# Group ends, norms and V's scaling on VectorE behind an attention's last unit, and two blocks of the next projection at a time

## The chip, the cores and the metric

The kernel runs on one core of one Trainium2 chip. The metric is the device time of one execution in microseconds (us), taken as the median of several runs.

## The reference

A network of four graph layers on one graph of 3327 nodes with 512 features. `adj` is sparse, with more neighbours for the nodes of low numbers. Every layer adds to x what it makes of the normed x:

```
h = max(layernorm(x), 0);  x = x + layer_l(h, adj)        # l = 0, 1, 2, 3
layers 0, 2, 3, attention with 8 heads of 64:
  Wh = h @ W;  e[i,j] = leaky_relu(s_dst[i] + s_src[j], 0.2) where adj[i,j] > 0
  out[i] = sum_j softmax_j(e[i,j]) * Wh[j]
  layer 0: out normed over the nodes, column by column, then relu;  layers 2, 3: elu(out)
layer 1, SAGE:
  agg = mean of h over the neighbours;  relu(([h W_self, agg W_nb] + b) @ W_comb + b_comb)
```

s_src and s_dst are products of Wh with two vectors for each head.

## The kernel before

The nodes are padded to 3328, which is 26 blocks of 128. A block has two groups of 64 destination rows, so there are 52 groups. For each group a list of neighbours is made once; a gather is an indirect DMA of 128 listed rows, issued by GpSimd.

**The attention** (`attend`, called for layers 0, 2 and 3) takes the groups in units of up to three gathers from the layer's `table`. A row of the table holds, for each head, V (64 numbers, already scaled with the exponential of the source's score) and that exponential itself, and the exponential for the other branch of the leaky relu. For a unit VectorE takes a maximum into PSUM (`mx`, L1266; three banks) and multiplies with the mask (`wgt`, L1273); TensorE then sums the weighted rows and their weights into `facc` (L1287). The first operand of the maximum, `r_bc` (L1198), comes from `r_dram` over `r_two` (L1190). The order of TensorE, VectorE and ScalarE within `attend` is by hand: instructions run in the order in which the program makes them. After each unit `later()` advances every open `ending` by one step, and calls `tick`.

An **ending** of a group copies its sums out of PSUM on ScalarE (`sums`, L1215), takes the reciprocal of the weights' sums on VectorE (`rd`, L1219), and multiplies on ScalarE, one head at a time (L1225), into `fhp`, or in layer 0 into `bn_y`. After a block's second group, `finish` follows: in layers 2 and 3 the elu and the sum with x (`fin_e` L1314, `fin_x` L1316 on ScalarE, L1318 and L1319 on VectorE, stored at L1320), then `proj.begin` for the next layer's projection. In layer 0, sums over the nodes follow (`bmean_ps` L1374, `bn_mean` L1376, `bn_d` L1401).

**SAGE** (layer 1) gathers rows of h (`z_rows`, issued at L1165), sums them with the mask on TensorE (`sage_acc`, L1522), and goes on with each block: scaled by the degree (`s_ag`, L1461), transposed (`a_ps` L1465, `aT` L1467), multiplied (`n_ps` L1471), `s_o` on VectorE (L1476, L1477), `proj.begin`. Here a scheduler orders the engines, after costs of its own.

**The next layer's projection** (`Following`) runs beside the layer before. `begin` opens a block's norm (`early`): sums and squares on ScalarE (`ln_j`, L782 and L784), the reciprocal root in short steps of both engines (L708 to L719), and `ln_h` on ScalarE (L792, L793). The other steps (`ready`) are `rest_by_rows` beside SAGE, and `rest` beside layer 2's attention. `rest`: four transposes (`p_ps` L845), `hT` with column sums on ScalarE (L848), the scores (`p_sd` L853; read at L857, L858, L860), `p_wh` (L866), V's scaling on ScalarE, one head at a time (L870), the store of the table's rows (L871), the transpose `p_tr` of the scores' exponentials (L874; halves at L730 to L734), and the store of `r_dram` (`r_row` L877, L879). `rest_by_rows` takes the scores from the products of `p_wh` (L808) with two vectors on VectorE (`sd_pr` L811, `sd_col` L813), scales V on VectorE (L824), and has `p_tr` at L831. `tick` advances the first open block by up to two steps; `drain` ticks until nothing is open. The PSUM tiles of `rest` share one bank (`pb=1`), those of `rest_by_rows` two. Layer 3's table is complete when `proj.drain()` ends behind `attend(2, ...)`, and layer 3's gathers come after it.

Of the kernel before, what the change touches and what calls it, by code (L numbers as in the profile page):

```python
# [23 lines left out]
F32 = mybir.dt.float32  # L24
# [8 lines left out]
ALU = mybir.AluOpType  # L33
# [5 lines left out]
P = 128  # L39
H = 8  # L40
F = 64
D = H * F
KC = D // P
BANK = 512
# [6 lines left out]
GB = 64  # L51
# [6 lines left out]
UNIT = 3  # L58
# [643 lines left out]
def rsqrt(nc, pool, cs, v, scale=1.0, bufs=3):  # L702


    n = v.shape[1]
    y = pool.tile([P, n], F32, name="rs_y", tag=f"rs_y{n}", bufs=bufs)
    g = pool.tile([P, n], F32, name="rs_g", tag=f"rs_g{n}", bufs=bufs)
    nc.scalar.activation(g, v, AF.Ln, scale=scale, bias=cs["eps"])  # L708
    nc.scalar.activation(y, g, AF.Exp, scale=-0.5)

    def step():
        h = pool.tile([P, n], F32, name="rs_h", tag=f"rs_h{n}", bufs=bufs)
        nc.vector.tensor_scalar(h, v, -0.5 * scale, -0.5 * EPS, ALU.mult, ALU.add)
        if n == 1:
            nc.vector.tensor_scalar(g, y, y, h, ALU.mult, ALU.mult)
        else:
            nc.vector.tensor_tensor(g, y, y, ALU.mult)
            nc.vector.tensor_tensor(g, g, h, ALU.mult)
        nc.vector.scalar_tensor_tensor(y, g, 1.5, y, ALU.add, ALU.mult)  # L719
        return y  # L720

    return step
# [17 lines left out]
class Following:  # L740
# [3 lines left out]
    def __init__(self, tc, cs, N, wl, W, WA, table, r_dram, pool, psum, pb=1, ab=None):  # L744

        self.__dict__.update(locals())
        nc = tc.nc
        if ab is not None:
            self.ab = pool.tile([P, 2, D], F32, name=f"ab{wl}")
            for k, a in enumerate(ab):  # L750
                nc.sync.dma_start(self.ab[:, k, :], a.partition_broadcast(P))
        self.NB = table.shape[0] // P
        self.Wt = pool.tile([P, KC, D], F32, name=f"fWt{wl}")
        nc.sync.dma_start(self.Wt, W.rearrange("(kc p) o -> p kc o", p=P))
        self.hs = pool.tile([P, self.NB, KC], F32, name=f"hs{wl}")
        self.early, self.ready = [], []

    def begin(self, c, xt):
        self.early.append(self.norm(c, xt))

    def tick(self):
        for _ in range(min(2, len(self.ready))):
            while self.ready and next(self.ready[0]) is None:
                self.ready.pop(0)
        for g in list(self.early):
            hx = next(g)
            if hx is not None:
                self.early.remove(g)
                self.ready.append((self.rest if self.ab is None else self.rest_by_rows)(*hx))
# [3 lines left out]
            self.tick()  # L773

    mean = Projection.mean

    def norm(self, c, xt):
        nc, pp, cs = self.tc.nc, self.pool, self.cs
# [62 lines left out]
    def rest(self, c, hx):  # L841
        nc, pp, WA, wl = self.tc.nc, self.pool, self.WA, self.wl
        tp = self.psum.tile([P, KC, P], F32, name="p_ps", tag="p_ps", bufs=self.pb)
        for kc in range(KC):
            nc.tensor.transpose(tp[:, kc, :], hx[:, kc * P : (kc + 1) * P], self.cs["ident"])  # L845
        hT = pp.tile([P, KC, P], F32, name="hT", tag="hT", bufs=2)
        for kc in range(KC):
            nc.scalar.activation(hT[:, kc, :], tp[:, kc, :], AF.Relu, accum_out=self.hs[:, c, kc : kc + 1])  # L848
        yield True
        self.mean(c, hT)  # L850
        sd = self.psum.tile([P, BANK], F32, name="p_sd", tag="p_ps", bufs=self.pb)
        for kc in range(KC):
            nc.tensor.matmul(sd[:, : 2 * H], hT[:, kc, :], WA[wl][:, kc, :], start=(kc == 0), stop=(kc == KC - 1))  # L853
        row = pp.tile([P, ROW], F32, name="v_row", tag="v_row", bufs=2)
        V = row[:, : H * (F + 1)].rearrange("p (h f) -> p h f", f=F + 1)
        d = sd[:, H : 2 * H]
        nc.scalar.activation(V[:, :, F : F + 1], d.rearrange("p (h o) -> p h o", o=1), AF.Exp)  # L857
        nc.scalar.activation(row[:, H * (F + 1) :], d, AF.Exp, scale=-0.8, bias=self.cs["down"])  # L858
        sf = pp.tile([P, H], F32, name="s_col", tag="s_col", bufs=2)
        nc.scalar.copy(sf, sd[:, :H])  # L860
        yield True

        nc.vector.tensor_scalar(sf, sf, -SMALL, SMALL, ALU.max, ALU.min)
        wh = self.psum.tile([P, D], F32, name="p_wh", tag="p_ps", bufs=self.pb)
        for kc in range(KC):
            nc.tensor.matmul(wh, hT[:, kc, :], self.Wt[:, kc, :], start=(kc == 0), stop=(kc == KC - 1))  # L866
        yield True
        rs = halves(nc, pp, self.cs, sf)
        for h in range(H):
            nc.scalar.mul(V[:, h, 0:F], wh[:, h * F : (h + 1) * F], V[:, h, F : F + 1])  # L870
        nc.sync.dma_start(self.table[c * P : (c + 1) * P, :ROW], row.bitcast(I32))  # L871
        yield True
        tr = self.psum.tile([2 * H, P], F32, name="p_tr", tag="p_ps", bufs=self.pb)
        nc.tensor.transpose(tr, rs(), self.cs["ident"])  # L874
        yield True
        rr = pp.tile([2 * H, P], F32, name="r_row", tag="r_row", bufs=2)
        nc.scalar.copy(rr, tr)  # L877
        n = P // GB
        nc.sync.dma_start(  # L879
            self.r_dram[c * n : (c + 1) * n, :, :, :].rearrange("g t h i -> (t h) g i"),  # L880
            rr.rearrange("h (g i) -> h g i", i=GB),
        )
        yield None
# [253 lines left out]
def sparse(ctx: ExitStack, tc: tile.TileContext, t: dict, out: bass.AP, WA, ls, cs, idx, rdeg, first):  # L1137
# [29 lines left out]
        )  # L1167


    def attend(layer, table, r_dram, finish, tick=lambda: None, home=None):  # L1170

# [8 lines left out]
        with tc.tile_pool(name=f"fatt{layer}", bufs=2) as ap, tc.tile_pool(  # L1182
            name=f"facc_ps{layer}", bufs=2, space=PSUM
        ) as aps, tc.manual_schedule(engines={ET.PE, ET.DVE, ET.Activation}):
            rows, rrs, rbs, accs, ends = {}, {}, {}, {}, []

            def fetch(g):
                if g < ls.G:
# [12 lines left out]
            def ending(g, hps={}):  # L1201

                b, u = divmod(g, PG)
                if u == 0:
                    hps[b] = home[:, b, :] if home is not None else None
                    if home is None:
                        hp_ = ap.tile([P, D], F32, name="fhp", tag="hp", bufs=3)
                        hps[b] = hp_
                hp, o0 = hps[b], u * GB
                fin = finish(b, hp, ap)  # L1210
                if u == PG - 1:
                    next(fin)
                yield
                sm = ap.tile([P, sw], F32, name="sums", tag="sums", bufs=4)
                nc.scalar.copy(sm, accs.pop(g)[:, :sw])  # L1215
                sm = sm.rearrange("p (q x) -> p q x", x=F + 1)
                yield
                rd = ap.tile([P, hq, 1], F32, name="rd", tag="rd", bufs=4)
                nc.vector.reciprocal(rd, sm[:, :, F : F + 1])  # L1219
                yield  # L1220
                for v in range(PG):
                    mine = slice(v * GB, (v + 1) * GB)
                    for q in range(hq):
                        h = q * PG + v
                        nc.scalar.mul(hp[o0 : o0 + GB, h * F : (h + 1) * F], sm[mine, q, 0:F], rd[mine, q, :])  # L1225
                yield
                if u == PG - 1:
                    del hps[b]
                    yield from fin
# [31 lines left out]
            for i, (g, k0, n, begins, stops) in enumerate(units):  # L1261
# [31 lines left out]
                            )  # L1293
                if stops:
                    ends.append(ending(g))
            while ends:
                later()

    def following(lx, layer, wl, W, pb=1, ab=None):
# [7 lines left out]
    def elu_into(xin, dst, then=lambda c, xt: None):  # L1307
        def finish(c, hp, pool):
            k = used(c) if dst is out else P
            xr = pool.tile([P, D], F32, name="fin_x", tag="fin_x", bufs=4)  # L1310
            nc.sync.dma_start(xr, xin[c * P : (c + 1) * P, :])
            ex = pool.tile([P, D], F32, name="fin_e", tag="fin_e", bufs=2)
            yield
            nc.scalar.activation(ex, hp, AF.Exp)  # L1314

            nc.scalar.activation(xr, xr, AF.Identity, bias=cs["less"])  # L1316
            yield
            nc.vector.scalar_tensor_tensor(xr, hp, 0.0, xr, ALU.max, ALU.add)  # L1318
            nc.vector.scalar_tensor_tensor(xr, ex, 1.0, xr, ALU.min, ALU.add)  # L1319
            nc.sync.dma_start(dst[c * P : c * P + k, :], xr[:k, :])  # L1320
            then(c, xr)

        return finish
# [206 lines left out]
    with ExitStack() as l3:  # L1530
        at2 = proj
        proj = following(l3, 3, 2, t["L3_gnn_W"])
        attend(2, at2.table, at2.r_dram, elu_into(x2, x3, proj.begin), proj.tick)
        proj.drain()
    attend(3, proj.table, proj.r_dram, elu_into(x3, out))


# [85 lines left out]
```

## Time and profile before

| what | value |
|---|---|
| median of three runs | 2559.43 us (2559.01 to 2560.68) |
| the profiled execution | 2553.76 us, span 2551.8 us, mean granted TensorE clock 0.851 |
| busy in the span | TensorE 1825.0 us, VectorE 1852.3 us, ScalarE 1068.3 us, GpSimd 1387.4 us |
| layer 0's end: sums read on ScalarE to `bn_mean` | 803.47 to 808.1 us |
| SAGE with the projection beside it | some 937 to 1445 us |
| join of layers 2 and 3: last attention matmul to layer 3's first gather | 1998.3 to 2046.5 us |
| layer 3's end: sums read on ScalarE to the last output step | 2532.65 to 2538.1 us |

The page shows one execution. A time in a timeline is in microseconds from the start of its span. Groups of instructions are shown as the source line, engine, operation and tile, then busy time, mean nanoseconds of one, the idle time of the engine in front of them, and what ended that idle time. PE is TensorE, PEld its weight loads, DVE VectorE, ACT ScalarE, POOL GpSimd, SP the engine that issues most DMAs. Block numbers in brackets, as in `p_wh`(23), count from 0 to 25.

### The profile page before, as it was taken

How to read it: one execution, taken by the hardware profiler on the slowest of the kernel's cores; microseconds unless marked ns; L12 is line 12 of the kernel's file. 1: busy time of each engine (PE TensorE's matmuls, PEld its weight loads, DVE VectorE, ACT ScalarE, POOL GpSimd, SP SyncE). 2: the span in 40 equal slices, each digit the busy share in tenths (PEclk: the TensorE clock that was granted, in tenths of full speed). 3: DMA queues.
4: the chain of work that ended last, by engine and by line, in shares of the span. 5: the costliest groups of instructions: out<-in, count | busy, mean ns of one | idle time of the engine just before them, and what ended most of it. 6: DMA issues, size and time to landing. Idle time of an engine off the chain costs nothing.

```text
span 2551.8 us, 53690 instructions
## 1 busy us (share of the span) xinstructions
PE 1825.0 (72%) x21112; PEld 1161.8 (46%) x21112; DVE 1852.3 (73%) x2272; ACT 1068.3 (42%) x3810; POOL 1387.4 (54%) x1482
## 2 busy tenths in 40 slices
PE   3667756776677698889999657778878646566653
PEld 2444444454454342223333356656555435555543
DVE  7667579999997850222333499999877279999996
ACT  4553212333445332334455214667766601233444
POOL 1000176777772026777777277776554067777672
PEclk9767889988888899999999778897877787777787
DMA  8773198888783566788888478887665178888784
GB/s 326 288 263 123 43 296 276 280 281 260 241 253 95 191 217 198 234 247 260 254 267 255 125 223 242 235 240 232 199 200 177 39 215 232 236 238 243 232 238 123
DMA packets 189057, 562.57 MB, mean 220 GB/s; under 512 B 37764, under 2 KB 42304, under 8 KB 185470
## 3 DMA queue, kind: packets, MB, share of 16 engines
q0 software_dynamic: 115456, 404.86, 53.3%
q1 hardware_dynamic: 73342, 154.20, 17.0%
q8 instruction: 169, 2.77, 0.4%
q14 instruction: 90, 0.74, 0.1%
HBM read 499.26 MB, written 59.68 MB: 219 GB/s over the span
## 4 chain that ended last, share of the span: by engine, by line
PE 30%; DVE 24%; issue 13%; ACT 9%; DMA 8%; POOL 3%; DVEq 0%; SPq 0%; POOLq 0%; ACTq 0%
DVE mx L1266 12%; PE facc L1287 8%; DVE wgt L1273 8%; PE sage_acc L1522 4%; DMA z_rows<-h_dram,idx 4%; PE p_wh L866 4%; DMA rows<-table,idx 3%; PE n_ps L1471 3%; PE p_wh L808 3%; ACT fhp L1225 2%; POOL z_rows L1165 2%; PE s_ps L1445 2%; POOL rows L1165 1%; ACT bn_y L1225 1%; ACT v_row L870 1%
## 5 line engine op out<-in xcount | busy, mean ns | idle before, releaser
L1165 POOL DMA_INDIRECT rows<-table,idx x1077 | 1027.7, 954 | 580.0 <-issue 224.5
L1287 PE MATMUL facc<-rows,wgt 128*64 128x65 f32 x17232 | 722.5, 253 | 393.7 <-DVE wgt L1273 259.7
L1287 PEld LDWEIGHTS facc<-rows,wgt 128*64 128x64 f32 x17232 | 667.1, 165 | 518.2 <-DVE wgt L1273 310.5
L1266 DVE TENSOR_TENSOR mx<-r_bc,rows 128x1536 f32<-128x1536 f32 (+1 forms) x405 | 639.4, 1579 | 48.4 <-DMA fin_x<-fx 17.7
L1273 DVE TENSOR_TENSOR wgt<-mx,mask 128x1536 f32<-128x1536 f32 (+1 forms) x405 | 638.4, 1576 | 42.3 <-DVE mx L1266 1.0
L1165 POOL DMA_INDIRECT z_rows<-h_dram,idx x359 | 340.7, 949 | 273.7 <-ACT hT L1442 141.0
L1225 ACT ACTIVATE fhp<-sums,rd 64x64 f32<-64x64 f32 x832 | 219.9, 334 | 305.4 <-DVE rd L1219 302.0
L1522 PE MATMUL sage_acc<-z_rows,z_mask 128*64 128x512 f32 x718 | 209.8, 618 | 33.0 <-DMA z_rows<-h_dram,idx 32.6
L1258 ACT ACTIVATE mask<-on 128x192 uint8<-128x192 uint16 (+1 forms) x135 | 46.5, 345 | 325.3 <-DVE on L1252 321.8
L1086 POOL DMA_DIRECT2D list_b<-shift x12 | 6.0, 503 | 271.7 <-DVE shift L1040 271.5
L811 DVE TENSOR_TENSOR sd_pr<-p_wh,ab 128x1024 f32<-128x1024 f32 x26 | 31.8, 1225 | 141.4 <-PE p_wh L808 141.4
L1522 PEld LDWEIGHTS sage_acc<-z_rows,z_mask 128*64 128x64 f32 x718 | 52.2, 137 | 156.2 <-issue 77.6
L680 PE MATMUL wh_ps<-fWt,hT 128*128 128x512 f32 x208 | 123.3, 748 | 0.0
L866 PE MATMUL p_wh<-fWt,hT 128*128 128x512 f32 x208 | 117.2, 714 | 1.4 <-ACT s_col L860 1.4
L1225 ACT ACTIVATE bn_y<-sums,rd 64x64 f32<-64x64 f32 x416 | 109.5, 333 | 2.4 <-DVE rd L1219 0.5
L1503 ACT CAST z_mask<-mask 128x128 f32<-128x128 uint8 (+1 forms) x196 | 52.7, 284 | 118.7 <-PE sage_acc L1522 117.5
L1476 DVE TENSOR_TENSOR s_o<-n_ps,bn_y 128x512 f32<-128x512 f32 x26 | 17.9, 690 | 116.2 <-PE n_ps L1471 116.2
L1215 ACT COPY sums<-facc 128x260 f32<-128x260 f32 x156 | 56.6, 363 | 104.7 <-DMA rows<-table,idx 77.7
L1471 PE MATMUL n_ps<-fWx,aT 128*128 128x512 f32 x208 | 98.7, 608 | 0.0
L808 PE MATMUL p_wh<-fWt,hT 128*128 128x512 f32 x208 | 96.9, 610 | 2.0 <-DVE hT L699 1.9
L1445 PE MATMUL s_ps<-fWx,hT 128*128 128x512 f32 x208 | 93.5, 603 | 3.4 <-ACT hT L1442 3.4
L1198 PE MATMUL r_bc<-r_two,fones 2*128 2x512 f32 x156 | 89.1, 575 | 6.6 <-DMA r_two<-r_dram 3.6
(213 smaller groups left out, 2146.3 us busy)
## 6 DMA issues: line engine op xcount, KB each, us to landing
adj_i<-in_adj SPq DMA_DIRECT2D x26, 1664.0 KB
table<-v_row SPq DMA_DIRECT2D x78, 264.0 KB
rows<-table,idx POOLq DMA_INDIRECT x1077
fin_x<-fx SPq DMA_DIRECT2D x52, 256.0 KB
ln_x<-in_x SPq DMA_DIRECT2D x26, 256.0 KB
bn_x<-in_x SPq DMA_DIRECT2D x13, 512.0 KB
fx<-bn_x SPq DMA_DIRECT2D x13, 512.0 KB
fsage_x<-fx SPq DMA_DIRECT2D x26, 256.0 KB
```

Of the source, the lines that this page charges most:

```text
L680: nc.tensor.matmul(wh, hT[:, kc, :], self.Wt[:, kc, :], start=(kc == 0), stop=(kc == KC - 1))
L808: nc.tensor.matmul(wh, hT[:, kc, :], self.Wt[:, kc, :], start=(kc == 0), stop=(kc == KC - 1))
L866: nc.tensor.matmul(wh, hT[:, kc, :], self.Wt[:, kc, :], start=(kc == 0), stop=(kc == KC - 1))
L1165: nc.gpsimd.indirect_dma_start(out=dst, out_offset=None, in_=src[:, :], in_offset=bass.IndirectOffsetOnAxis(ap=idx[:, k : k + 1], axis=0))
L1198: nc.tensor.matmul(rb, ones[0:2, :].bitcast(F32R), rrs.pop(g).bitcast(F32R), start=True, stop=True)
L1225: nc.scalar.mul(hp[o0 : o0 + GB, h * F : (h + 1) * F], sm[mine, q, 0:F], rd[mine, q, :])
L1266: nc.vector.tensor_tensor(mx[:, :n], rbs[g].unsqueeze(1).to_broadcast(full), gt[:, :n, H * (F + 1) : ROW].unsqueeze(3).to_broadcast(full), ...
L1273: nc.vector.tensor_tensor(wt[:, :n], mx[:, :n], mk.unsqueeze(2).to_broadcast(full), ALU.mult)
L1287: nc.tensor.matmul(accs[g][v * GB : (v + 1) * GB, q * (F + 1) : (q + 1) * (F + 1)], wt[:, k, h, :], gt[:, k, h * (F + 1) : (h + 1) * (F + 1)],
L1445: nc.tensor.matmul(ps, hT[:, kc, :], Wx[:, 0, kc, :], start=(kc == 0), stop=(kc == KC - 1))
L1471: nc.tensor.matmul(ps, aT[:, kc, :], Wx[:, 1, kc, :], start=(kc == 0), stop=(kc == KC - 1))
L1522: nc.tensor.matmul(acc[u * GB : (u + 1) * GB, :], m, z, start=f, stop=l)
```

## The change

Behind the last unit of an attention, endings that have not yet read their sums do all of their work on VectorE: a reciprocal straight from PSUM and two products with a broadcast operand, one for each half of the partitions. `begin` takes a norm from VectorE's column statistics (`norm_by_columns`) where the projection has `ab`, which is the one beside SAGE, for all its blocks, or where the spare banks are open. In the attention of layer 2, which now gets the projection as `beside`, one more tile of the maxima's three banks is taken behind the last unit and given to the projection (`hurry`): `p_sd`, `p_wh` and `p_tr` then go to its banks 0, 1 and 2, `tick` advances each of up to two open blocks by one step, and V is scaled by one product on VectorE. The projection's remaining steps run in `attend`'s last loop, within its order by hand, in place of `proj.drain()`.

```diff
     def begin(self, c, xt):
-        self.early.append(self.norm(c, xt))
+        self.early.append((self.norm_by_columns if self.spare is not None or self.ab is not None else self.norm)(c, xt))
+    def busy(self):
+        return self.early or self.ready
+    def hurry(self, spare):
+        self.spare = spare
+    def bank(self, shape, name, k):
+        if self.spare is not None:
+            return self.spare[: shape[0], k, : shape[1]]
+        return self.psum.tile(shape, F32, name=name, tag="p_ps", bufs=self.pb)
     def tick(self):
+        if self.spare is not None:
+            for g in self.ready[:2]:
+                if next(g) is None:
+                    self.ready.remove(g)
+            self.step()
+            return
         for _ in range(min(2, len(self.ready))):
             while self.ready and next(self.ready[0]) is None:
                 self.ready.pop(0)
+        self.step()
...
+    def norm_by_columns(self, c, xt):
+        nc, pp, cs = self.tc.nc, self.pool, self.cs
+        st = pp.tile([P, nc.vector.BN_STATS_DIM], F32, name="ln_st", tag="ln_st", bufs=2)
+        nc.vector.bn_stats(st, xt)
+        mv = pp.tile([P, nc.vector.BN_AGGR_DIM], F32, name="ln_mv", tag="ln_mv", bufs=3)
+        nc.vector.bn_aggr(mv, st)
+        step = rsqrt(nc, pp, cs, mv[:, 1:2])
+        yield
+        y = step()
+        if c == self.NB - 1:
+            nc.vector.tensor_tensor(y, y, cs["real"], ALU.mult)
+        hx = pp.tile([P, D], F32, name="ln_h", tag="ln_h", bufs=3)
+        nc.vector.tensor_scalar(hx, xt, mv[:, 0:1], y, ALU.subtract, ALU.mult)
+        yield c, hx
...  rest():
-        sd = self.psum.tile([P, BANK], F32, name="p_sd", tag="p_ps", bufs=self.pb)
+        sd = self.bank([P, BANK], "p_sd", 0)
...
-        wh = self.psum.tile([P, D], F32, name="p_wh", tag="p_ps", bufs=self.pb)
+        wh = self.bank([P, D], "p_wh", 1)
...
-        for h in range(H):
-            nc.scalar.mul(V[:, h, 0:F], wh[:, h * F : (h + 1) * F], V[:, h, F : F + 1])
+        if self.spare is not None:
+            nc.vector.tensor_tensor(
+                V[:, :, 0:F], wh.rearrange("p (h f) -> p h f", f=F), V[:, :, F : F + 1].to_broadcast([P, H, F]), ALU.mult
+            )
+        else:
+            for h in range(H):
+                nc.scalar.mul(V[:, h, 0:F], wh[:, h * F : (h + 1) * F], V[:, h, F : F + 1])
...
-        tr = self.psum.tile([2 * H, P], F32, name="p_tr", tag="p_ps", bufs=self.pb)
+        tr = self.bank([2 * H, P], "p_tr", 2)
...  attend(..., beside=None), in ending():
+                if over:
+                    sm = accs.pop(g)[:, :sw].rearrange("p (q x) -> p q x", x=F + 1)
+                    rd = ap.tile([P, hq, 1], F32, name="rd", tag="rd", bufs=4)
+                    nc.vector.reciprocal(rd, sm[:, :, F : F + 1])
+                    for v in range(PG):
+                        mine = slice(v * GB, (v + 1) * GB)
+                        nc.vector.tensor_tensor(
+                            hp[o0 : o0 + GB, :].rearrange("p (q v f) -> p q v f", v=PG, f=F)[:, :, v, :],
+                            sm[mine, :, 0:F],
+                            rd[mine].to_broadcast([GB, hq, F]),
+                            ALU.mult,
+                        )
+                    if u == PG - 1:
+                        del hps[b]
+                        yield from fin
+                    return
...
-            while ends:
+            over.append(True)
+            if beside is not None:
+                mx = aps.tile([P, UNIT, H, GB], F32, name="mx", tag="mx", bufs=1)
+                beside.hurry(mx.rearrange("p k h i -> p k (h i)"))
+            while ends or (beside is not None and beside.busy()):
                 later()
...
-        attend(2, at2.table, at2.r_dram, elu_into(x2, x3, proj.begin), proj.tick)
-        proj.drain()
+        attend(2, at2.table, at2.r_dram, elu_into(x2, x3, proj.begin), proj.tick, beside=proj)
```

More of the change, by code (lines that the diff above doesn't have):

```diff
@@ L755, in __init__ @@
         self.hs = pool.tile([P, self.NB, KC], F32, name=f"hs{wl}")
-        self.early, self.ready = [], []
+        self.early, self.ready, self.spare = [], [], None
     def begin(self, c, xt):
-        self.early.append(self.norm(c, xt))
-    def tick(self):
+        self.early.append((self.norm_by_columns if self.spare is not None or self.ab is not None else self.norm)(c, xt))
[7 more added lines that the diff above has]
+        return self.psum.tile(shape, F32, name=name, tag="p_ps", bufs=self.pb)
+    def tick(self):
+        if self.spare is not None:
[4 more added lines that the diff above has]
+            return
         for _ in range(min(2, len(self.ready))):
@@ L764, in tick, with step @@
                 self.ready.pop(0)
+        self.step()
+    def step(self):
         for g in list(self.early):
@@ L1167, in gather, with attend @@
         )
-    def attend(layer, table, r_dram, finish, tick=lambda: None, home=None):
+    def attend(layer, table, r_dram, finish, tick=lambda: None, home=None, beside=None):
         width = table.shape[1]
@@ L1184, in attend @@
         ) as aps, tc.manual_schedule(engines={ET.PE, ET.DVE, ET.Activation}):
-            rows, rrs, rbs, accs, ends = {}, {}, {}, {}, []
+            rows, rrs, rbs, accs, ends, over = {}, {}, {}, {}, [], []
             def fetch(g):
```

## The prediction

> **What bounds the kernel now.** I read the chain of the page first, then each place that the diff touches in the timeline and the waits.
>
> ```profile
> PE 30%; DVE 24%; issue 13%; ACT 9%; DMA 8%; POOL 3%; DVEq 0%; SPq 0%; POOLq 0%; ACTq 0%
> ...
> L1225 ACT ACTIVATE fhp<-sums,rd 64x64 f32<-64x64 f32 x832 | 219.9, 334 | 305.4 <-DVE rd L1219 302.0
> ...
> L1215 ACT COPY sums<-facc 128x260 f32<-128x260 f32 x156 | 56.6, 363 | 104.7 <-DMA rows<-table,idx 77.7
> ```
>
> ACT has 9% of the chain: most of its 220 us of `fhp` lies beside other work. What the change takes off ACT counts only where nothing runs beside it, behind the last unit of a layer. The longest such place is the join of layers 2 and 3, in the waits from 1996 to 2060:
>
> ```profile
> POOL rows L1165 <- DMA r_two<-r_dram: 67.4, 1, 67.4
> ```
>
> Layer 3's first gather stands until the last block of the projection has stored its row. In the chain of that window one block is:
>
> ```profile
> 2003.74 1.90 PE p_sd L853 x8
> ...
> 2006.11 5.48 PE p_wh L866 x8
> 2011.61 1.75 ACT v_row L870 x8
> 2013.36 0.02 issue
> 2013.38 1.06 ACT fhp L1225 x4
> 2014.44 0.03 issue
> 2014.47 1.05 ACT fhp L1225 x4
> ...
> 2015.54 0.30 ACT ln_s L792
> ```
>
> The reader is to see a serial alternation: weight matmuls on PE, then ACT with V's eight products, then with eight ends of a group, then the next norm, and PE waits. Three blocks lie behind the last unit; tables go out at 2013.38, 2030.22 and 2043.56, the last row at 2044.18, the gather at 2046.52.
>
> Layer 0's end is ACT alone too, the last group's ends behind those of the group before:
>
> ```profile
> 801.42 2.14 ACT L1225 ACTIVATE bn_y<-sums,rd 64x64 f32<-64x64 f32 x8 [0.24 <-DVE rd L1219]
> ...
> 803.47 0.35 ACT L1215 COPY sums<-facc 128x260 f32<-128x260 f32 x1
> 803.85 0.18 DVE L1219 RECIPROCAL rd<-sums 128x4 f32<-128x4 f32 x1 [2.47 <-ACT sums L1215]
> 804.07 2.14 ACT L1225 ACTIVATE bn_y<-sums,rd 64x64 f32<-64x64 f32 x8 [0.25 <-DVE rd L1219]
> ```
>
> SAGE (937 to 1445) is limited by gathers first (a gather every 1.25 us). From 1308 on PE is the bound: 67.08 of 70 us busy from 1330 to 1400, a block every 13.5 us, and this wait in each of the last blocks (waits of PE, 1000 to 1425):
>
> ```profile
> PE sage_acc L1522 <- DMA z_rows<-h_dram,idx: 26.3, 17, 3.1
> PE p_tr L831 <- DVE r_half L734: 4.1, 7, 0.6
> ```
>
> **What the Trainium skill says.** "ScalarE: Activation LUTs", What ACT_TABLE_LOAD costs: 186 ns + 0.833 per element, and 93 more for a per-partition pointer. With 64 elements and one pointer that is an estimate of 332 ns; the row has 334. So a group end is eight fixed costs, which one wide instruction saves. "VectorE: DVE Perf Modes", The perf-mode tier table: a single-source fp32 operation from SBUF runs two elements a cycle, tensor_tensor and anything from PSUM one. The trace agrees where it shows them: tensor_tensor 128x512 from PSUM took 687 ns (L636), tensor_scalar from PSUM 0.69 us (L1376). "TensorE: Matmul & The Clock Gate", Part 1: PE runs at half clock after an idle window. In the join each `p_wh` begins with matmuls 0.85 us apart, and eight took 5.47 to 6.00 us, against 3.60 in SAGE; they stay slow if PE still waits.
>
> **The change part by part.**
>
> (a) Ends of the last group, once in each of three attentions. Out: COPY 0.36, eight products 2.14. In: a reciprocal from PSUM, 0.17 to 0.20 by L1219, and two tensor_tensor 64 x 256. That shape is not shown; 128x1024 takes 1.225 and 128x1536 1.76, so 0.27 per 256 and 0.155 fixed: 0.42 (0.69, the 512 row, at worst). Together 1.1 us, with DVE free. Layer 0: PE's sums end at 802.13, so DVE is done at 803.2; `bmean` then waits for ACT's products of the group before, which end at 803.56, and starts at 803.6 instead of 806.25: **-2.6** (2.0 to 3.0). Behind it bn_mean and bn_d follow in series. Layer 3: now DVE's 2532.16 (end of L1319), done 2533.25, then exp and fin_x on ACT 1.25, the two DVE steps 1.45: 2535.95 instead of 2538.11: **-2.15** (1.8 to 2.4). The output's store follows directly.
>
> (b) The norm by column statistics, for all 26 SAGE blocks and the two last blocks of layer 3's projection. Out on ACT: 0.63, 0.19, 0.20, 0.72, 0.19, 0.29 and 0.81 = 3.0 us. In on DVE: statistics 0.68 (L599), aggregate 0.18 (L600), tensor_scalar 0.43 (estimate from the page on VectorE, Side-by-side: where the cycles go: 256 cycles at two elements each and some 150 fixed, at 0.96 GHz) to 0.69. ACT is some 55% busy in SAGE's end and DVE 38%, so neither bounds it. The order of PE's work bounds it, and it moves: `p_wh` of block k comes ahead of `n_ps` of k+1, and behind `n_ps` stand four sage matmuls, `p_tr`, five sage matmuls, and then `p_ps` of k+1. So `p_tr` gets work ahead of it, and its 0.59 us wait goes. What may be late next is `ln_h` for `p_ps`. Its path from `n_ps`: s_o 1.43 (L1476, L1477), statistics 0.9, ln and exp 0.29 + 0.20 and gaps 0.15, the Newton steps 0.55, ln_h 0.43 to 0.69, in sum 3.95 to 4.2, and up to 0.3 behind `r_half` of the block before on DVE. Cover on PE: nine sage matmuls of 0.455 and 0.28 = 4.4. I take 0.15 of new wait, so 0.43 over the 7 blocks with that wait: -3.0 (0 to -4.1). If the cover were gone the whole 4.4 would lie open. The drain loses some: today the last `p_wh` starts 16.74 behind the last sage matmul; in the new order the last `n_ps` stands behind the `p_wh` before it and ends 9.6 behind instead of 6.5, the faster norm gives back 2.1, so +1.0. SAGE: **-2.0** (+1 to -3.1). POOL can't hide this: it stands idle for PE 0.92 us more than its usual 0.30 in each of the last 8 blocks.
>
> (c) The join. The spare banks are one tile, the maxima's: a write into any bank waits for the readers of the others as they come in program order. I followed the instruction order with today's durations. `hT`(23) ends at 2003.69 as before. Then the eight products of group 50, exp and fin_x stand in front of `s_col`(23) on ACT, so `p_wh`(23) starts at 2007.42, **1.3 later** than now. It ends at 2012.9 (5.47, half clock); V's scaling on DVE is done at 2013.65 (0.69 instead of 1.75). `ln_h`(24) has been ready since 2010, so p_ps, hT (1.1), p_sd (1.9, from 2015.75), s_col and p_tr(23)'s read follow: `p_wh`(24) at 2018.33 instead of 2022.72, ends 2023.6. It waits for ACT's read of `p_tr`(23), the same tile; behind it on PE stands p_ps(25), whose hT nobody else could start. p_ps(25), hT to 2025.35, mean, p_sd to 2027.9, `p_wh`(25) at 2028.63 instead of 2035.76. At 5.3 to 6.0 it ends by 2034.2; scaling 0.7, table at 2034.9, p_tr 0.28, r_row 0.25, r_dram at 2035.5 instead of 2044.18: **-8.7**. The two blocks hardly overlap; the gain is that 2.14 of ends, 1.1 of scaling and 1.5 of norm no longer stand between two `p_wh`. Bounds: 6 if bank waits or DVE's queue (fin_x, scaling, norm) cost one more us a block; 10.5 if PE stays warm for a block. Its DMAs keep their order on SP, and POOL's order is the same. From the row on 2.34 us to the gather stay.
>
> Sum: -2.6 -2.15 -2.0 -8.7 = -15.45. The profiled execution took 2553.76 (span 2551.8 and 2.0 around it), 5.67 (0.22%) under the median of 2559.43. It gives 2538.3 for such an execution; against the median I predict **2544** (-0.60%). Own range, adding the bounds: 8.8 to 19, so 2540 to 2551.
>
> **The rivals.**
> Rival A, the join only half: DVE's strict order and the one-tile dependency put each block's matmuls behind the other's readers, and the three ACT items ahead of `s_col` cost their 1.3 without return. For it: two blocks share one PE queue. Against: the ACT work removed is on the chain, seen above. It gives 4 of the 8.7, and 2544 + 4.7 = 2549; with SAGE at +1 too, 2552.
> Rival B, slower: in SAGE the norm comes late for `p_ps`. All of it is on DVE now, and if sd_pr, sd_col and v_row (1.23 + 1.21 + 0.69 = 3.1) run ahead of it, its path is 7.3 against the 4.4 of cover: 2.9 of wait for 0.59 saved, +2.3 on the 8 blocks where PE is the bound, and, where the gathers have only a little slack, on the 5 before: +30, +1 of drain, -13.45 elsewhere: 2577; with the 8 blocks alone, 2565. It decides from about 1.6 us a block over 8. Against it: in the instruction order s_o and the norm stand together, ahead of the next sd_pr.
> Rival C, no change to measure: the ends gain only their own 4.75, and what follows each (the bn variance, the first rows of layer 3) waits for transfers: 2555. Against: the first gather's wait names the row alone.
> That the change doesn't do what it says: only the last group, and in the third attention only blocks 24 and 25 of norms, take the new path; this is in the sum.
>
> **How the numbers follow.** Forecast 0.60, A 0.18, C 0.10, B 0.12. 0.2%, what a measurement of this kernel tells from no change, is 5.1 us: faster means under 2554.3. Forecast and A are faster, C is split, mostly no change: faster 0.78, same 0.10, slower 0.12. Range: from 2538 (own 2540, with 2 for the runs' own spread) to 2555, which leaves B out and a little at each end.
>
> **What would show it.** Layer 0: `bmean` directly behind ACT's eight products of group 50, no second COPY. SAGE: p_tr without a wait, the period under 13.3, and any wait of `p_ps` for ln_h; that wait over 0.6 makes step (b) wrong. Join: from the last attention matmul to the row's store 37 us instead of 45.9, V's scaling 0.7; `p_wh` starts as given. If `p_wh` of two blocks stand next to each other, or lie 13 apart, step (c) is wrong. The prediction falls if the time is over 2554.

## The result and the profile after

The changed kernel takes 2547.12 us (median of 5; 2544.94 to 2550.44), the kernel before on the same chip 2560.23 (2559.01 to 2565.69). The ratio is 0.9954 (95% interval 0.9937 to 0.9970): 0.46% faster, 12 us with 8 to 16 in the interval. The forecast was 2544.

Where it comes from is read between landmarks that both traces have (the profiled executions: 2553.76 and 2547.12 us):

| stretch | before, us | after, us | difference |
|---|---|---|---|
| layer 0: last attention matmul to `bn_mean` | 5.29 | 2.65 | -2.64 |
| SAGE: first gather to last `sage_acc` matmul | 487.8 | 493.5 | **+5.8** |
| last `sage_acc` matmul to layer 2's first gather | 29.8 | 30.0 | +0.2 |
| join: last attention matmul to layer 3's first gather | 48.20 | 36.10 | **-12.1** |
| layer 3: last attention matmul to the issue of the last output store | 6.94 | 4.78 | -2.16 |
| start, the three attentions and the rest, which the change leaves alone | | | +4.3 |

The four places sum to -10.9, within the interval of the ratio. The last row is variation between executions: the first gather came at 319 us in one profile and 322 in the other, and layer 0's attention took 482.7 and 484.8 (482.3 to 482.8 in most of the other runs below).

Layer 0's end, in the timeline of the changed kernel:

```profile
806.40 2.14 ACT L1284 ACTIVATE bn_y<-sums,rd 64x64 f32<-64x64 f32 x8 [0.25 <-DVE rd L1278]
...
807.18 0.18 DVE L1260 RECIPROCAL rd<-facc 128x4 f32<-128x4 f32 x1 [0.81 <-PE facc L1346]
807.40 0.88 DVE L1263 TENSOR_TENSOR bn_y<-facc,rd 64x256 f32<-64x256 f32 x2
...
808.59 1.12 PE L1437 MATMUL bmean_ps<-bn_y,fones 127*128 127x512 f32 x2 [0.43 <-ACT bn_y L1284]
```

The second COPY and the second eight products are gone; VectorE's 1.1 us lie beside ScalarE's eight products of the group before, and the matmul waits for those, as in the forecast.

The join, TensorE's timeline in the changed kernel (start, duration, operation, count, and the wait in front in brackets):

```profile
2015.18 5.86 PE L903 MATMUL mx<-fWt,hT 128*128 128x512 f32 x8 [2.44 <-ACT s_col L897]
2020.88 0.60 PE L882 MATMUL p_ps<-fident,ln_h 128*128 128x128 f32 x4
2023.31 0.28 PE L916 MATMUL mx<-fident,r_half 128*16 128x128 f32 x1 [1.83 <-DVE r_half L734]
2023.43 0.96 PE L890 MATMUL mx<-WA,hT 128*128 128x16 f32 x8
2024.99 3.70 PE L903 MATMUL mx<-fWt,hT 128*128 128x512 f32 x8 [0.61 <-ACT r_row L919]
...
2032.67 5.40 PE L903 MATMUL mx<-fWt,hT 128*128 128x512 f32 x8 [0.61 <-ACT r_row L919]
```

The three `p_wh` now start 9.8 and 7.7 us apart, before 16.6 and 13.0. The next block's transposes stand directly behind `p_wh`(23), and `p_wh`(24) took 3.70 us, at full clock: the row of stretches shows a granted clock of 1.00 from 2021 to 2028.6.

```profile
2005.75:2021.00 15.25, 8.82 (x22) 4.99 (x23) 6.66 (x17) 9.32 (x36) 0.00 (x0) 0.66 0.10 37
2021.00:2028.60 7.60, 5.16 (x23) 2.87 (x22) 2.13 (x8) 2.16 (x14) 0.00 (x0) 1.00 0.10 38
```

(Columns: window, length, busy time and count on PE, PEld, DVE, ACT and POOL, then the granted clock, the DMA share, GB/s.)

SAGE is the surprise. One block of its last part on TensorE, before:

```profile
1340.28 3.60 PE L1471 MATMUL n_ps<-fWx,aT 128*128 128x512 f32 x8
1343.72 3.60 PE L808 MATMUL p_wh<-fWt,hT 128*128 128x512 f32 x8
1347.24 3.65 PE L1522 MATMUL sage_acc<-z_rows,z_mask 128*64 128x512 f32 x16
...
1351.96 0.28 PE L831 MATMUL p_tr<-fident,r_half 128*16 128x128 f32 x1 [0.58 <-DVE r_half L734]
...
1352.27 1.08 PE L1522 MATMUL sage_acc<-z_rows,z_mask 128*64 128x512 f32 x4
```

and after:

```profile
1347.21 1.07 PE L1585 MATMUL sage_acc<-z_rows,z_mask 128*64 128x512 f32 x2
1348.22 3.70 PE L1534 MATMUL n_ps<-fWx,aT 128*128 128x512 f32 x8
1351.85 1.94 PE L1585 MATMUL sage_acc<-z_rows,z_mask 128*64 128x512 f32 x8
1353.72 0.28 PE L868 MATMUL p_tr<-fident,r_half 128*16 128x128 f32 x1
1353.92 2.79 PE L1585 MATMUL sage_acc<-z_rows,z_mask 128*64 128x512 f32 x10
```

The wait for `r_half` is gone, TensorE waits for nothing in these blocks, and a block takes longer: 14.17 us instead of 13.50. The counts tell why. Two records of `sage_acc` alone take 1.07 us, and four take 1.08. A matmul of SAGE uses 64 columns of the array and comes as two records; the two groups of a block use the two halves. The starts within these stretches are:

```
before, 16 records: +0.007, +0.473, +0.007, +0.423, +0.006, +0.423, +0.007, +0.422 ...
after, the 2 records: +0.480, then n_ps after +0.523
after, last 4 of the 10 records: ... +0.422, +0.007, +0.423 (alone), +0.429 (alone)
```

Two matmuls on different halves start 7 ns apart and share their time; one that stands alone takes all of it, 0.86 us. The Trainium skill has this in "TensorE: Matmul & The Clock Gate", Part 3: Packing small matmuls; it gives some 4 ns between the starts, this trace shows 7. The scheduler's new order puts `p_ps`, `a_ps` and `p_wh` between the two matmuls of one pair: the first closes the ten records, its partner stands alone ahead of `n_ps`.

### The profile page after: what moved, and what is told of

It is laid out like the page before. It is cut to its first block, busy times and chain, and to the rows that moved or that the text cites. A ratio compares the mean times of both kernels' runs of the same rounds, so it can differ in the third digit from the quotient of the medians.

```text
span 2545.3 us, 53533 instructions
## 1 busy us (share of the span) xinstructions
PE 1862.1 (73%) x21112; PEld 1187.9 (47%) x21112; DVE 1900.7 (75%) x2365; ACT 989.4 (39%) x3563; POOL 1385.8 (54%) x1482
## 5 line engine op out<-in xcount | busy, mean ns | idle before, releaser
L1346 PE MATMUL facc<-rows,wgt 128*64 128x65 f32 x17232 | 753.0, 259 | 366.6 <-DVE wgt L1332 239.9
L1346 PEld LDWEIGHTS facc<-rows,wgt 128*64 128x64 f32 x17232 | 697.0, 171 | 493.6 <-DVE wgt L1332 292.0
L1585 PE MATMUL sage_acc<-z_rows,z_mask 128*64 128x512 f32 x718 | 219.1, 621 | 31.2 <-DMA z_rows<-h_dram,idx 30.8
L845 PE MATMUL p_wh<-fWt,hT 128*128 128x512 f32 x208 | 97.1, 610 | 2.1 <-DVE hT L699 1.9
L903 PE MATMUL p_wh<-fWt,hT 128*128 128x512 f32 x184 | 97.6, 677 | 0.0
L1043 PE MATMUL words_ps<-wsel,adj_b 128*128 128x8 bf16 x676 | 24.6, 168 | 87.3 <-DVE adj_b L1025 47.6
```

What stands on the lines that cost most here:

```text
L1346: nc.tensor.matmul(accs[g][v * GB : (v + 1) * GB, q * (F + 1) : (q + 1) * (F + 1)], wt[:, k, h, :], gt[:, k, h * (F + 1) : (h + 1) * (F + 1)],
L1585: nc.tensor.matmul(acc[u * GB : (u + 1) * GB, :], m, z, start=f, stop=l)
```

## The experiments

Theory P: SAGE's 5.8 us come from the parted pair. Rivals: V, they are variation between executions; N, the norm on VectorE costs by itself. For the join, theory J: ScalarE's work gone from between the `p_wh` is most of the gain; rival T: two blocks at a time are the gain.

**SAGE's norm on ScalarE again, the rest as changed.**

```diff
-(self.norm_by_columns if self.spare is not None or self.ab is not None else self.norm)
+(self.norm_by_columns if self.spare is not None else self.norm)
```

> The changed kernel with the projection beside SAGE normed on ScalarE again; group ends and join stay as changed. Theory P (in the changed kernel's order of TensorE one pair of SAGE's matmuls in each block is parted: the two halves of 64 columns no longer start together, and each takes 0.86 us alone): the order is that of before again, a block takes 13.50 us instead of 14.17, from SAGE's first gather to its last matmul 487.8 instead of 493.5 us, and the total is 5 to 6 us under the changed kernel, near 2541. Rival V (SAGE's 5.8 us are variation between executions, like the 2.8 us before the first gather): as the changed kernel, 2547.

Measured: 2539.27 us, ratio to before 0.9922 (0.9902 to 0.9942). The period, the time from one block to the next in the last part of SAGE, is 13.50 us again, and SAGE takes 488.4 us. V falls. This kernel is the changed one without its harmful part. The run takes the norm and the new order away together, so it doesn't tell P from N.

**The pairs kept together, norm on VectorE.**

```diff
-            zs.sort(key=lambda x: x[:2])
+            zs.sort(key=lambda x: (x[0], -x[1]))
```

> The changed kernel, norm on VectorE beside SAGE kept; only, in each pair of SAGE's matmuls the group whose gather comes later is multiplied first, so that the scheduler has no reason to part the two. Theory P: the parted pair's 0.86 us per block goes, the period falls from 14.17 to 13.3 or, if the wait of p_tr is gone for nothing, 12.9; over some 12 blocks 10 us, total 2537 to 2540. Rival N (the norm on VectorE itself costs, by its path or by contention): the period stays at 14.1, total 2547.

Measured: 2541.88 us, ratio 0.9930 (0.9910 to 0.9949). SAGE took 491.8 us, the period 14.00: neither 13.3 nor 14.17. By the trace no pair is parted in these blocks (8, 8 and 4 records), so 0.86 us are back, but waits came in their place:

```profile
1350.29 1.94 PE L1585 MATMUL sage_acc<-z_rows,z_mask 128*64 128x512 f32 x8
1352.75 0.44 PE L1528 MATMUL a_ps<-fident,s_ag 128*128 128x128 f32 x2 [0.53 <-ACT s_ag L1524]
1353.35 0.63 PE L837 MATMUL p_ps<-fident,ln_h 128*128 128x128 f32 x4 [0.16 <-DVE ln_h L811]
```

TensorE is through with the sums sooner, and now `s_ag` on ScalarE and `ln_h` on VectorE are late. The trace shows why: the norm's logarithm (L708) could start on ScalarE at 1350.69, but stands behind a cast of a mask that waits for TensorE's sums, and starts at 1351.60; `s_ag` stands behind both. So `ln_h` is ready 4.9 us behind `n_ps`, in the changed kernel 4.05. P was right on the pair and wrong on what its repair brings, 1.7 of SAGE's 5.8 us. N holds in this sense, that with whole pairs the norm on VectorE still costs SAGE 4.0 us (a period of 14.00 against 13.50).

**The norm on VectorE beside SAGE alone, on the kernel before.** The edit takes the group ends' new path, the spare tile and the join's loop out of the changed kernel, so that of the condition in `begin` only `self.ab is not None` can be true.

> The kernel before with one part of the change, the norm on VectorE beside SAGE; group ends and join as before. Theory P: the same order of TensorE as the changed kernel, period 14.17, total 5 to 6 us above before, near 2566. The forecast on record: 2 us under before, 2558.

Measured: 2561.01 us, ratio 1.0015 (1.0004 to 1.0025); period 14.17, SAGE 494.2 us, 6.4 more than before in the profiles. Alone, this part makes the kernel slower. The medians lie 2.8 us apart and the ratio gives 1 to 6 us: less than the 5 to 6 expected, which the interval only just reaches.

**Pairs parted with nothing moved between engines.**

```diff
-            zs.sort(key=lambda x: x[:2])
+            zs.sort(key=lambda x: (x[1], x[0]))
...
-                if r != at:
-                    at = r
-                    tick()
+                if u == 0:
+                    tick()
```

> The kernel before, norms on ScalarE; only the order of SAGE's matmuls within a part of four is by group and not by pair, which by the built order leaves an odd number (3 and 7) between other matmuls in each of the last blocks. Theory P, with nothing moved between engines: one matmul more stands alone in each of two stretches, +0.86 us a block, period near 14.4, total 8 to 11 us above before, near 2570. Rival N: parted pairs cost nothing, period 13.5, total 2560.

Measured: 2570.21 us, ratio 1.0052 (1.0035 to 1.0068), period 14.25. A block on TensorE shows the odd counts (14 records and 6, of which one matmul each has no partner):

```profile
1358.58 3.65 PE L1521 MATMUL sage_acc<-z_rows,z_mask 128*64 128x512 f32 x14
...
1363.51 1.93 PE L1521 MATMUL sage_acc<-z_rows,z_mask 128*64 128x512 f32 x6
```

Fourteen take what sixteen took before, and six take what eight take. The edit also moves the ticks, but over a block `sage_acc` takes 5.45 us instead of 4.60 and the wait for `r_half` is 0.1 shorter, which is the 0.75 of the period. The loss is there without any norm on VectorE: that a parted pair costs a matmul's 0.86 us is shown.

**One block at a time with the spare banks.**

```diff
-            for g in self.ready[:2]:
+            for g in self.ready[:1]:
```

> The changed kernel, but with the spare banks tick advances one open block, not two. From the last matmul of layer 2's attention to layer 3's first gather it is 48.2 us before and 36.1 in the changed kernel. Theory J (most of the gain is ScalarE's work gone from between two p_wh, and the two blocks only hide the transposes and hT of the next block): 37.5 to 39. Rival T (two blocks at a time are the gain, TensorE staying warm with it): 42 or more.

Measured: 2546.93 us in a single execution, as in the next three runs; join 37.47 us. T, which asks for 42 or more, falls. That two blocks at a time are worth the other 1.4 us is not shown, because the join varies by as much from execution to execution. Two of the runs above have the changed kernel's join as it stands: with SAGE's norm on ScalarE it took 36.12 us, with the pairs kept 37.66. In the latter, block 24's `p_sd` and `p_wh` are:

```profile
2017.89 1.49 PE L890 MATMUL mx<-WA,hT 128*128 128x16 f32 x8
2019.98 6.17 PE L903 MATMUL mx<-fWt,hT 128*128 128x512 f32 x8 [0.61 <-ACT r_row L919]
```

The waits in front are the same as in the changed kernel (1.83 for `r_half`, 0.61 for `r_row`), but `p_wh`(24) took 6.17 us instead of 3.70, at a granted clock of 0.63 from 2017 to 2026.2. So 1.5 us between two single joins may be the clock of one execution alone.

**Blocks 24 and 25 normed on ScalarE.**

```diff
-(self.norm_by_columns if self.spare is not None or self.ab is not None else self.norm)
+(self.norm_by_columns if self.ab is not None else self.norm)
```

> The changed kernel, but blocks 24 and 25 of layer 3's projection are normed on ScalarE as before; SAGE keeps its norm on VectorE. In the changed kernel ln_h(24) is ready 3.3 us before its transposes start and ln_h(25) 5.3 us, so theory J expects little: join 36 to 38. Rival: ScalarE's 3.0 us of norm stand ahead of s_col and hT of the block in work, twice, 41 or more.

Measured: 2550.64 us; join 43.85 us, 7.75 longer. Theory J's "little" was wrong, and the rival's 41 or more holds: the norm on VectorE carries much of the join's gain.

```profile
2019.13 0.28 PE L916 MATMUL mx<-fident,r_half 128*16 128x128 f32 x1 [1.69 <-DVE r_half L734]
2019.24 0.60 PE L882 MATMUL p_ps<-fident,ln_h 128*128 128x128 f32 x4
2022.24 1.89 PE L890 MATMUL mx<-WA,hT 128*128 128x16 f32 x8 [2.40 <-ACT r_row L919]
2024.61 6.52 PE L903 MATMUL mx<-fWt,hT 128*128 128x512 f32 x8 [0.48 <-ACT s_col L897]
```

`ln_h`(24)'s transposes come only behind `p_tr`(23), and TensorE waits in front of `p_tr` and again in front of `p_sd`. It stays near half clock (0.57 granted from 2019 to 2031): the three `p_wh` took 6.57, 6.52 and 6.00 us instead of 5.86, 3.70 and 5.40, and the three `p_sd` 1.89, 1.89 and 1.62 instead of 1.89, 0.96 and 1.03. That is 4.1 + 1.5 = 5.6 of the 7.75, and 2.1 are left for the waits. How much of the 5.6 the norm's place causes stays open: 0.7 of it lies in `p_wh`(23), ahead of what the norm can delay, and with nothing moved in the join these matmuls were 2.0 us slower in the execution with the pairs kept than in the changed kernel's. My expectation read the slack of `ln_h` off the trace and left out TensorE's clock.

**V scaled on ScalarE behind the last unit too.**

```diff
-        if self.spare is not None:
+        if False:
             nc.vector.tensor_tensor(
```

> The changed kernel, but V is scaled by eight products on ScalarE behind the last unit too, reading the spare bank. Theory J: 1.75 instead of 0.69 us for the last block, and hT of the next block queued behind the products twice, 1.75 each: join 39.5 to 41. Rival (V's scaling only counts in the last block): 37.2.

Measured: 2552.14 us; join 41.49 us, 5.4 longer, a little over the expected. But `p_wh` and `p_sd` of the three blocks are slower by 3.9 of the 5.4. What is left, 1.5, is less than the 4.6 that the expectation summed.

**Three tiles in place of one.**

```diff
     def bank(self, shape, name, k):
-        if self.spare is not None:
-            return self.spare[: shape[0], k, : shape[1]]
+        if self.spare is not None and k == 1:
+            return self.spare.tile(shape, F32, name="r_bc", tag="r_bc", bufs=2)
+        if self.spare is not None and k == 0:
+            return self.spare.tile([P, UNIT, H, GB], F32, name="mx", tag="mx", bufs=1).rearrange("p k h i -> p k (h i)")[: shape[0], 0, : shape[1]]
...
-                mx = aps.tile([P, UNIT, H, GB], F32, name="mx", tag="mx", bufs=1)
-                beside.hurry(mx.rearrange("p k h i -> p k (h i)"))
+                beside.hurry(aps)
```

> The changed kernel, but p_sd, p_wh and p_tr lie in three tiles of their own (the maxima's, one of r_bc's two, the projection's own bank) and not in one, so that none waits for a reader of another. In the changed kernel p_wh(24) and p_wh(25) each wait 0.61 us for r_row's read of p_tr. Theory: the join loses these, 36.1 to 35. Rival (the dependency on one tile is what keeps two blocks from overlapping): 33 or less.

Measured: 2543.01 us; join 31.96 us, 4.1 less, where 1.1 was expected; the rival's side. `p_wh`(24) and `p_wh`(25) took what they took in the changed kernel (3.68 and 5.38), so this is not the clock. TensorE in this kernel:

```profile
2010.93 1.89 PE L892 MATMUL mx<-WA,hT 128*128 128x16 f32 x8 [0.46 <-ACT hT L887]
2012.66 5.43 PE L905 MATMUL r_bc<-fWt,hT 128*128 128x512 f32 x8
2017.93 0.60 PE L884 MATMUL p_ps<-fident,ln_h 128*128 128x128 f32 x4
```

I had counted the two waits of 0.61 us for `r_row`. The larger one was in front of `p_wh`(23): 2.44 us for `s_col`, which in the changed kernel must read its bank of the tile, behind eight products and an elu on ScalarE, before any bank may be written. With tiles of its own `p_wh`(23) follows `p_sd`(23) at once.

**The group before the last on VectorE too, one tile.** In an ending whose sums are already copied when the last unit is over:

```diff
                 yield
+                if over:
+                    for v in range(PG):
+                        mine = slice(v * GB, (v + 1) * GB)
+                        nc.vector.tensor_tensor(
+                            hp[o0 : o0 + GB, :].rearrange("p (q v f) -> p q v f", v=PG, f=F)[:, :, v, :],
+                            sm[mine, :, 0:F],
+                            rd[mine].to_broadcast([GB, hq, F]),
+                            ALU.mult,
+                        )
+                    yield
+                    if u == PG - 1:
+                        del hps[b]
+                        yield from fin
+                    return
                 for v in range(PG):
```

This kernel has SAGE's norm on ScalarE.

> As the first of these, but p_sd, p_wh and p_tr in the maxima's one tile: SAGE's norm on ScalarE, and the products of the group before the last on VectorE. ScalarE's 2.14 us ahead of s_col(23), which p_wh(23) waits for in the one tile, go: p_wh(23) starts 7.3 instead of 9.4 us behind the last attention matmul, join 34 instead of 36.1. Rival: p_wh(24) waits for its own block's norm and the join stays at 36.

Measured: 2536.58 us in a single execution; join 35.45 us. `p_wh`(23) starts 8.17 us behind the last attention matmul instead of 9.43, not 7.3, and half of that is lost again, since it ran near half clock throughout (6.48 us, 0.55 granted). What is left, 0.6, is less than the join varies, so the rival, that nothing is gained, stands.

**All of it together:** SAGE's norm on ScalarE, three tiles, both groups' ends on VectorE.

> Everything the runs point to: the changed kernel with SAGE's norm on ScalarE, p_sd, p_wh and p_tr in tiles of their own, and behind the last unit the products of the group before the last on VectorE too, read from its copied sums. Theory: SAGE as before (13.50 a block, 488 us), join 30 to 31.5 us (32.0 with tiles apart, less what ScalarE's 2.14 us ahead of fin_e and s_col were worth), ends of layers 0 and 3 as in the changed kernel or 0.3 shorter. Total 5 us under the changed kernel with SAGE's norm on ScalarE: 2534 to 2535, ratio to before 0.990. Rival (TensorE falls back to half clock in the shorter join and takes the gain back): join 34, total 2537.

Measured: 2530.72 us (median of 5) against 2556.97, ratio 0.9896 (0.9880 to 0.9912); join 29.86 us, SAGE 13.50 a block. That is under the 2534 to 2535 expected, and the rival falls. By the ratios its gain on the kernel before is about twice the change's. Layer 0's end took 2.38 us, 0.3 shorter, as expected. Layer 3's end took 5.50 us there, 0.7 longer than in the changed kernel and not 0.3 shorter: there VectorE does these products (0.86 us) behind the last steps of the block before, and the last group's behind them.

**The same with SAGE's norm on VectorE and the pairs kept.**

> The same, but SAGE's norm stays on VectorE and the pairs are kept together by taking the group whose gather comes later first: period 14.0, SAGE some 3.5 us longer than in the run with the norm on ScalarE. Total 2537 to 2538.

Measured: 2531.67 us, ratio 0.9899 (0.9884 to 0.9914), again under the expected. The period is 14.00, SAGE 490.1 us against 486.2 in the run above, but the medians differ by 1 us only, less than the intervals.

**The group ends alone, on the kernel before.** The edit leaves of the change the list `over` and its branch in `ending`.

> The kernel before with the group ends on VectorE alone; norms, V's scaling and the drain of the projection as before. Theory: from the last attention matmul to bn_mean 2.65 us in layer 0 (5.3 to 6.2 before), to the last output step 4.8 in layer 3 (6.9 before), and in the join the last group's eight products leave the chain, 48.2 less 2.1 to 2.5, so 46. SAGE 488 us, 13.50 a block. Total 7 to 8 us under before, ratio 0.997. Rival (in the join the ends on VectorE are hidden anyway, or hold up fin_x): join 48, total 5 us under before.

This run came to another chip, on which the kernel before takes 2957.89 us and TensorE's clock was 0.782. Measured: 2946.98, ratio 0.9961 (0.9942 to 0.9980). Layer 0's end took 2.64 us and layer 3's 4.79, as expected. The total is 5 to 17 us under before by the interval, where 7 to 8 were expected. The join took 47.32, but no trace of the kernel before was taken on that chip, so the join's share of this part stays open.

## Why the prediction was right, and where it was not

That the total came out close is in part luck: two errors of opposite sign stood in the sum, +8.0 us in SAGE and -3.4 in the join.

Step (a) held as worked out. Layer 0: -2.6 forecast, -2.64 measured; layer 3: -2.15 and -2.16. The two products over 64 x 256 took 0.88 us together, 0.42 each by the estimate. In two runs without this part the same end took 6.24 us instead of 5.29: `bmean` took 2.07 us instead of 1.13, at a granted clock of 0.50 instead of 1.00, behind the same wait of 3.07. Against such an execution the part is worth 3.6.

Step (b) failed: -2.0 forecast, +6.0 measured. The step said that the order of TensorE's work moves, and costed the move by its waits alone. The waits came out as forecast: `p_tr` no longer waits, and `p_ps` does not wait for `ln_h`. What failed is the term left at nothing, TensorE's own work for a block; it shows in the sentence "nine sage matmuls of 0.455", an average over whole pairs, used where the new order parts one. Over a block: sage_acc 4.60 to 5.59 (+1.0), `n_ps` and `p_wh` with a change of array width in front of or behind each 6.96 to 7.26 (+0.3), `a_ps` and `p_tr` with its wait 1.44 to 0.83 (-0.6), in sum the +0.68 that the period shows. The pair is not all of it. With whole pairs the step would still have failed: that kernel's SAGE took 4.0 us more than before and not 2.0 less. The forecast took neither ScalarE nor VectorE for a bound, and its path of `ln_h` left out what stands ahead of the logarithm in ScalarE's queue. In the changed kernel that path took 4.05 us, as worked out; with the pairs kept it took 4.9. Rival B put a loss in the same place, but by another mechanism, a late `ln_h`, and from 1.6 us a block; in the changed kernel `ln_h` was in time, and the block lost 0.68. The drain was +0.2 and not +1.0.

Step (c) was right in kind and too small: -8.7 forecast, -12.1 measured. `p_wh`(23) started 1.63 us later than before (1.3 forecast), and layer 3's first gather came 36.1 us behind the last attention matmul (39.5 forecast). The term that was mis-sized is TensorE's speed: `p_wh`(24) was taken at 5.3 us and took 3.70, `p_sd` of blocks 24 and 25 at 1.9 and took 0.96 and 1.03. That is 3.4 us, as large as the whole difference; what else was off, each less than 0.6 us, cancels out. The forecast took the slow clock of the kernel before for its middle ("they stay slow if PE still waits") and had a warm TensorE only in its bound of 10.5, for one block; the measured gain lies beyond that bound. As the execution with the pairs kept shows, up to 1.5 us of the gain may be the clock of the one execution that was profiled. Rival A fell. Its premise, that the one tile holds the blocks back, is true and worth 4.1 us, but those were never in the forecast's gain.

By parts, each undone alone, the join was longer by 7.75 us for the norm on VectorE, 5.4 for V's scaling and 1.4 for two blocks at a time, each from a single execution. The first two are clear of the 1.5 us by which the join varied and don't add up to 12.1: in both, slower matmuls are most of the loss. The third is not clear of it.

## What to carry to other kernels

Before a step is moved to an idle engine under a scheduler, read what the new order does to instructions that only are cheap next to a partner, not only what it does to waits: a TensorE that waits for nothing may still take longer. In a stretch where TensorE waits between blocks, look at the clock of the matmuls behind a wait as well as at the wait, and look at several executions: here the same matmuls behind the same waits took 3.70 us in one and 6.17 in another. And give results that go to different readers tiles of their own, even where one tile has the banks.

## What was not expected of the hardware

A change between matmuls 128 and 64 columns wide cost TensorE 0.14 to 0.20 us at each edge: starts stand 0.52 us apart across it and the next 0.47 or 0.53, against 0.42 to 0.43 within a stretch. From `n_ps` to `p_wh`, both 128 wide, they stand 0.43 apart. "TensorEngine Tiling (Array Packing)", Key Properties, of the Trainium skill says that a change of tiling mode drains TensorE; no run here shows the drain itself, and this would be its size.

`tensor_scalar` over 128x512 fp32 from SBUF with two per-partition operands (`ln_h`) took 0.55 to 0.56 us in 24 of its 28 instructions in the changed kernel, at most 0.67, between the prediction's estimate of 0.43 and the 0.69 of the `tensor_scalar` from PSUM (`bn_mean`).

The kernel before took 2557 us on one chip and 2958 on another. The one trace from the slower chip is of the kernel with the group ends alone: there the attention's matmuls averaged 268 ns and VectorE waited 157 us for them, against 253 ns and 1 us in the trace of the kernel before. Why the chips differ stays open.
